# Two images' last layers side by side in a four-image, four-layer network kernel

## The chip, the cores and the metric

The kernel runs on one core of a Trainium2 chip. The measure is the device time of one execution in microseconds (us), here the median of three runs. The program takes all four images in one launch, in fp32.

The engines are named as in the profile: PE is TensorE's matrix products and PEld its loads of weights, DVE is VectorE, ACT is ScalarE, POOL is GpSimd, and SP is SyncE, which here mostly issues transfers. Each engine takes its own instructions strictly in the order in which the program lists them, and waits on semaphores for what other engines make.

## What is computed

An input of 4 x 32 x 32 x 384 goes through four residual layers, each of the form x + f(gn(x)), where gn is a group norm over 32 groups:

```python
# layer 0: deformable attention, 6 heads of 64, with a sampled position bias
offset = tanh(einsum('bhwc,ct->bhwt', gelu(ln(conv(q))), w_offp)) * [H/2, W/2]
xs = bilinear_sample(xg, offset + ref)
attn = softmax(q @ (xs @ w_k).T * scale + bilinear_sample(rpe, disp))
x = x + (attn @ (xs @ w_v)) @ w_out
# layer 1: attention, 12 heads of 32, weighted by similarity to group centres
sim = sigmoid(beta + alpha * l2norm(xg) @ l2norm(gc).T)
attn = softmax(q @ k.T * scale) * ((sim @ sim.T) * gamma + 1 - gamma)
x = x + (attn / (attn.sum(axis=2) + 1e-8) @ v) @ Wproj
# layer 2: box sums, 5 along W and 20 along the channels
s, d = box5(xn), box20(box5(xn * xn))
x = x + box20(s * s) / (d * norm)
# layer 3: 3 x 3 outlook attention
attn = softmax((xn @ Wa + ba).reshape(B, H, W, 9, 9))
x = x + fold3x3(attn @ patches3x3(xn @ Wv))
```

An image has 1024 tokens (N) of 384 channels (C), kept as three blocks (KC = 3) of 128 partitions by 1024. Images do not depend on each other.

## The kernel before

Two classes hold the work of an image. `Front` does layer 0; `Trunk` does layers 1, 2 and 3. A front leaves its result in a DRAM tensor `x1[b % 2]` (L489 and L495 store it), and a trunk loads it from there. Image 0's front runs by itself. From then on `Net.layer3` (L293) runs the trunk of image b with the front of image b + 1 woven in. Both are Python generators: each `yield` hands back a number of units for the work just issued, and the order of these yields is the order in which every engine gets its instructions. A trunk has 1109 units (`TRUNK_STEPS`): 15 for the norm, 158 for `inputs1`, 118 for each of six pairs, 18 for `out1`, 93 for `layer2`, 117 for `layer3`. A front has 714 (`FRONT_STEPS`). `done` counts the trunks in whole images and `ahead` the fronts; after each trunk step, front steps are issued until `ahead` is at least `done + LEAD`, with LEAD = 0.1. So the front of the next image is through when a trunk stands at 0.9 of its units, in its layer 2. After image 2's trunk there is no front left, and image 3's trunk runs alone.

The stages of a trunk, in order:

- `start` (L1285) loads `x1` into the buffer `whole` (three transfers on SP) and the matrix `gmat`, which sums over the groups, into a weight slot. For image b + 1 it is called in image b's `layer3`, at L2005, before the last products of that layer.
- `image` (L1292): the group norm, in place. Its statistics are on DVE (L328, L329), a product with `gmat` on PE (L362), a square root on ACT (L378) and the normalisation on DVE (L386).
- `layer1` (L1306): `inputs1` (L1319) makes queries, keys, values and group features (L407, L1356, L421), the first denominators and the similarities (L1572). Then six `pair`s (L1586) of heads follow: L1518 scores for the row sums, L1653 scores, L1661 exponentials on ACT, L1683 group weights, L1690 their product on DVE, L1625 the product with the values. A pair's result goes to the DRAM tensor `yd`; pair 5 reads the results of the earlier pairs back into `q4`, `k4` and `xg`, and its own result goes to `xg` by L1732 at its end.
- `layers23` (L1734) opens a pool for the remaining scopes. In it `out1` (L1742) loads x again, multiplies by `Wproj` (L1757) and adds (L1769). `layer2` (L1775) has the norm, box sums along W on DVE (L1792, L1811 to L1816), transposes into PSUM (L1799) and box sums over the channels as products with a band matrix (L1824); the quotient goes through ACT (L1839, L1840, L1849, L1850) and DVE (L1844 to L1867). `layer3` (L1872) has the norm, the 81 attention logits (L1889), their softmax (L1914, L1916), the values (L421), a product with `sel` (L1954), a passage through DRAM that turns the 3 x 3 attention into a band of tokens (`skew`, L1987, and `mt`, L1989), the band products (L2012) and the stores (L2021).

What the two streams share: the weight tiles of 128 x 3 x 384 come from one pool of three slots, in the order of the calls of `weights` (L253, on SP's queue); PSUM has two "big" buffers of 128 x 1024 and four "bank" buffers of 128 x 512. Box sums, transposes, scores and dense products take "big"; nearly all else takes "bank". Front tiles live on one side of SBUF and trunk tiles on the other. `whole` is a single buffer in the pool `keep`, used by each image in turn.

In the front, a half-head has eight steps of bias (L906, L907, L911, L912), score products (L918) with DVE additions (L921, L925), a row maximum, then L951, L952 and the products with the values (L953); a front has 12 half-heads. Its end is the division by the denominators, the output projection (the L407 products with `qpad` as left operand) and the stores to `x1`. It begins with norm, query, convolution, positions, gathers on POOL, and the key and value products (L407, L421).

Of the kernel before, what the change touches and what calls it, by code (L numbers as in the profile page):

```python
# [27 lines left out]
NB, HW, C = 4, 32, 384  # L28
N = HW * HW
KC = C // P  # L30
# [29 lines left out]


EARLY = (12, 0, 14, 8, 8)
TRUNK_STEPS, FRONT_STEPS, LEAD = 1109.0, (714.0, 714.0, 714.0), 0.1


def bc(ap, axis, n):
# [7 lines left out]
class Net:  # L74
# [217 lines left out]

    def layer3(self, b, out):  # L293

        for w in self.trunk.image(b, out):
            self.done += w / TRUNK_STEPS
            while self.ahead < self.done + LEAD:
                self.ahead += next(self.fronts, 1.0)
        assert self.ahead >= min(b + 1, NB - 1)


class Lane:
# [937 lines left out]
class Early(Front):  # L1240
# [14 lines left out]
    def begin(self, b):  # L1255
        nc = self.nc
        with self.scope("l0p"), self.tc.tile_pool(
            name=self.nm("l0w"), bufs=2, side=self.side
        ) as self.wts:
            self.qpad = self.wt([P, KC, PW, PW], "qpad")  # L1260
            nc.gpsimd.memset(self.qpad, 0.0)
            xh = yield from self.normed(b)
            for ko in range(KC):
                self.project(xh, ko, self.wq)
                yield
            self.taps[1] = self.conv_weights(1)
            oT = self.wt([P, KC, 2, N // 2], "a12", 2)
            for k in range(KC):
                yield from self.convolve(oT, k)
            nc.sync.dma_start(self.qp1, self.qpad.rearrange("p k y x -> p (k y x)"))  # L1270
            nc.sync.dma_start(self.of1, oT.rearrange("p k g n -> p (k g n)"))


class Trunk(Lane):
# [15 lines left out]
        self.begun = x, self.weights("gmat")  # L1290

    def image(self, b, out):  # L1292
        x, gmat = self.begun
        self.norm(x, x, None, gmat)
        self.xh = x
        yield 15
        with self.scope("l1y"):


            self.q4, self.k4 = self.wt([P, N], "q4"), self.wt([P, N], "k4")  # L1300
            self.xg = self.wt([P, N], "xg")
            yield from self.layer1(b)
            yield from self.layers23(b, out)


    def layer1(self, b):  # L1306
# [279 lines left out]
    def pair(self, p):  # L1586
# [5 lines left out]
        qa, ka = self.qks[p % 2]  # L1592
        sim = self.sim
        if p == 5:

            for k, t in enumerate((self.q4, self.k4, self.xg[0:64, :])):
                nc.sync.dma_start(t, self.yd[k * P : k * P + t.shape[0], :])
# [130 lines left out]
        y = self.wt([P, 512], "y")  # L1728
        nc.scalar.copy(y, av)
        out = self.yd[p * 64 : (p + 1) * 64, :] if p < 5 else self.xg[64:P, :]  # L1730
        for h in range(2):
            nc.sync.dma_start(out[:, h * 512 : (h + 1) * 512], y[64 * h : 64 * h + 64, :])  # L1732

    def layers23(self, b, out):  # L1734
        with self.scope("l23"):
            whole, self.x = self.whole()
            self.spare = whole[:, KC * N :].rearrange("p (y x) -> p y x", y=HW)
            yield from self.out1(b)
            yield from self.layer2()
            yield from self.layer3(b, out)  # L1740

    def out1(self, b):  # L1742
        nc, v = self.nc, self.nc.vector
        for k in range(KC):
            nc.scalar.dma_start(self.x[:, k, :], self.x1[b % 2][k * P : (k + 1) * P, :])
        w = self.weights("Wproj")
        y = (self.q4, self.k4, self.xg)
        self.mv = [self.moments() for _ in range(2)]

        ps = {}  # L1750

        def part(ko, ks):
            if ko not in ps:
                ps[ko] = self.big()
            for h in range(2):
                for ki in ks:
                    nc.tensor.matmul(  # L1757
                        ps[ko][:, h * 512 : (h + 1) * 512],
                        w[:, ki, ko * P : (ko + 1) * P],
                        y[ki][:, h * 512 : (h + 1) * 512],  # L1760
                        start=ki == 0,
                        stop=ki == KC - 1,
                    )

        part(0, (0, 1))
        part(1, (0, 1))
        for ko in range(KC):
            part(ko, (2,) if ko < 2 else (0, 1, 2))
            v.tensor_tensor(self.x[:, ko, :], ps[ko], self.x[:, ko, :], ALU.add)  # L1769
            self.stats(self.mv[0], self.x, ko)  # L1770
            yield 6
# [100 lines left out]
    def layer3(self, b, out):  # L1872
        nc, v = self.nc, self.nc.vector
        skew = self.skew[b % 2]
        with self.scope("l3"):
# [5 lines left out]
            w = self.weights("Wv")  # L1881
# [120 lines left out]
                    )  # L2002
                nc.scalar.copy(ys[:, i], pt[:, 0:C])
            yield 20
            if b + 1 < NB:  # L2005
                self.start(b + 1)
            for i in range(NJ):
                ps = self.bank()
# [10 lines left out]
                y = ys[:, i]  # L2019
# [87 lines left out]
```

## Time and profile before

| | |
|---|---|
| runs, median of 3 | 4391.65 us (4374.2 to 4397.6) |
| profiled execution | 4362.05 us |
| its span, first to last instruction | 4360.0 us |
| mean granted TensorE clock | 0.950 |
| transfers over the span | 391.18 MB, mean 90 GB/s |

The largest groups of instructions on the page, in the form "line, engine, operation, out <- in, shapes, count, then busy time and mean duration, then idle time of the engine just ahead of them with what ended it":

```profile
L1683 PE MATMUL bank<-whole,sg 128*128 128x512 f32 (+3 forms) x2304 | 850.1, 499 | 2.5 <-POOL sg L1636 1.0
...
L1690 DVE SCALAR_TENSOR_TENSOR e<-bank,gam,e 128x512 f32<-128x512 f32 x768 | 560.0, 747 | 304.5 <-PE bank L1683 188.0
...
L1653 PE MATMUL big<-qa,ka 64*128 64x512 f32 x1536 | 454.9, 672 | 85.6 <-ACT big L1528 82.4
...
L953 PE MATMUL bank<-lg,va 128*128 128x512 f32 x576 | 270.2, 611 | 12.8 <-ACT lg L952 12.8
...
L907 DVE SCALAR_TENSOR_TENSOR z<-win,bias_f,z 128x528 f32<-128x528 f32 x288 | 214.6, 762 | 20.6 <-ACT z L906 19.1
```

PE is the engine that is busiest. L1683 and L1653 belong to layer 1's pairs, L953 and L907 to layer 0's half-heads. Mean durations are times from start to end of one instruction; products overlap on PE, so that a group's busy time is less than its count times its mean.

### The profile page before, as it was taken

How to read it: one execution, taken by the hardware profiler on the slowest of the kernel's cores; microseconds unless marked ns; L12 is line 12 of the kernel's file. 1: busy time of each engine (PE TensorE's matmuls, PEld its weight loads, DVE VectorE, ACT ScalarE, POOL GpSimd, SP SyncE). 2: the span in 40 equal slices, each digit the busy share in tenths (PEclk: the TensorE clock that was granted, in tenths of full speed). 3: DMA queues.
4: the chain of work that ended last, by engine and by line, in shares of the span. 5: the costliest groups of instructions: out<-in, count | busy, mean ns of one | idle time of the engine just before them, and what ended most of it. 6: DMA issues, size and time to landing. Idle time of an engine off the chain costs nothing.

```text
span 4360.0 us, 45308 instructions
## 1 busy us (share of the span) xinstructions
PE 3915.6 (90%) x14832; PEld 1676.8 (38%) x14832; DVE 3107.4 (71%) x5902; ACT 2305.8 (53%) x3640; POOL 962.7 (22%) x979
## 2 busy tenths in 40 slices
PE   5888889998999898989899989899989989999998
PEld 3333433333334443433333444333333334344444
DVE  3599676878787547687878746678787874566654
ACT  3266445666674334576666433366675641566633
POOL 0655242112121105221212101431121301000000
PEclk8999989999999998999999999899999999999999
DMA  8744253123221255321222145432221214311111
GB/s 183 237 124 123 83 175 104 47 57 88 60 77 49 85 162 161 104 66 41 81 60 81 40 143 142 140 104 63 55 83 44 78 33 137 103 40 28 33 33 44
DMA packets 297461, 391.18 MB, mean 90 GB/s; under 512 B 168002, under 2 KB 229710, under 8 KB 296714
## 3 DMA queue, kind: packets, MB, share of 16 engines
q1 hardware_dynamic: 244826, 221.57, 18.1%
q0 software_dynamic: 39936, 145.53, 11.0%
q10 hardware_dynamic: 12464, 21.19, 1.5%
q8 instruction: 118, 1.93, 0.2%
q14 instruction: 117, 0.96, 0.1%
HBM read 300.15 MB, written 88.32 MB: 89 GB/s over the span
## 4 chain that ended last, share of the span: by engine, by line
PE 48%; DVE 26%; ACT 9%; issue 9%; DMA 4%; POOL 4%; SPq 0%; ACTq 0%; DVEq 0%; POOLq 0%
PE bank L1683 10%; PE big L1653 6%; PE big L407 5%; DVE nmax L1527 4%; DVE e L1690 3%; PE bank L953 3%; ACT big L1528 3%; PE bank L421 3%; PE big L1518 3%; POOL gat L769 2%; PE bank L1678 2%; PE bank L1625 2%; DVE z L1072 2%; DVE z L907 2%; PE big L656 2%
## 5 line engine op out<-in xcount | busy, mean ns | idle before, releaser
L1683 PE MATMUL bank<-whole,sg 128*128 128x512 f32 (+3 forms) x2304 | 850.1, 499 | 2.5 <-POOL sg L1636 1.0
L1690 DVE SCALAR_TENSOR_TENSOR e<-bank,gam,e 128x512 f32<-128x512 f32 x768 | 560.0, 747 | 304.5 <-PE bank L1683 188.0
L1528 ACT ACTIVATE big<-big,nmax 128x1024 f32<-128x1024 f32 x384 | 417.5, 1087 | 295.3 <-DVE nmax L1527 293.5
L1683 PEld LDWEIGHTS bank<-whole,sg 128*128 128x128 f32 x2304 | 399.4, 196 | 349.7 <-issue 273.5
L1653 PE MATMUL big<-qa,ka 64*128 64x512 f32 x1536 | 454.9, 672 | 85.6 <-ACT big L1528 82.4
L1527 DVE TENSOR_REDUCE nmax<-big 128x1 f32<-128x1024 f32 x384 | 452.3, 1217 | 61.4 <-PE big L1518 61.2
L1661 ACT ACTIVATE e<-big 128x1024 f32<-128x1024 f32 x384 | 381.8, 1020 | 175.4 <-PE big L1653 165.3
L894 POOL DMA_INDIRECT win<-strips,widx x288 | 312.8, 1086 | 702.7 <-DVE z L907 384.6
L1636 POOL TENSOR_SCALAR sg<-whole,gam 128x512 f32<-128x512 f32 x192 | 150.9, 786 | 1336.4 <-PE bank L1683 1058.3
L1518 PE MATMUL big<-k,q 32*128 32x512 f32 x1536 | 271.7, 657 | 41.7 <-ACT big L1528 31.3
L953 PE MATMUL bank<-lg,va 128*128 128x512 f32 x576 | 270.2, 611 | 12.8 <-ACT lg L952 12.8
L1653 PEld LDWEIGHTS big<-qa,ka 64*128 64x128 f32 x1536 | 147.2, 198 | 345.8 <-ACT big L1528 178.5
L769 POOL DMA_INDIRECT gat<-pairs,sidx x192 | 213.3, 1111 | 301.3 <-DVE ix_one L548 165.0
L912 DVE SCALAR_TENSOR_TENSOR lg<-z,bias_f,lg 128x512 f32<-128x512 f32 x288 | 216.6, 769 | 49.1 <-ACT lg L911 47.4
L906 ACT ACTIVATE z<-win,bias_f 128x528 f32<-128x528 f32 x288 | 205.4, 736 | 58.1 <-DVE lg L912 26.5
L951 DVE TENSOR_TENSOR lg<-lg,tb 128x512 f32<-128x512 f32 x288 | 182.0, 690 | 74.5 <-ACT tb L944 74.5
L907 DVE SCALAR_TENSOR_TENSOR z<-win,bias_f,z 128x528 f32<-128x528 f32 x288 | 214.6, 762 | 20.6 <-ACT z L906 19.1
L1625 PE MATMUL bank<-e,vs 128*32 128x512 f32 x1536 | 211.6, 619 | 15.9 <-DVE vs L1619 15.9
L1695 ACT COPY gn<-bank 128x128 f32<-128x128 f32 (+2 forms) x288 | 106.3, 370 | 208.5 <-DVE e L1690 207.6
L911 ACT ACTIVATE lg<-z,bias_f 128x512 f32<-128x512 f32 x288 | 199.9, 717 | 17.0 <-DVE z L907 13.8
L921 DVE TENSOR_TENSOR lg<-bank,lg 128x512 f32<-128x512 f32 x288 | 191.2, 682 | 11.7 <-PE bank L918 11.0
L918 PE MATMUL bank<-qs,kz 64*128 64x512 f32 x288 | 169.4, 672 | 12.4 <-DVE e L1690 9.0
(321 smaller groups left out, 6301.1 us busy)
## 6 DMA issues: line engine op xcount, KB each, us to landing
q<-qd SPq DMA_DIRECT2D x48, 256.0 KB
xg<-xgd SPq DMA_DIRECT2D x48, 256.0 KB
w<-in_gmat SPq DMA_DIRECT2D x16, 576.0 KB
pairs<-gat SPq DMA_DIRECT2D x48, 192.0 KB
w<-in_w_off SPq DMA_DIRECT2D x12, 576.0 KB
w<-in_Wqkv SPq DMA_DIRECT2D x12, 576.0 KB
a<-in_x SPq DMA_DIRECT2D x16, 384.0 KB
x<-a ACTq DMA_DIRECT2D x4, 1536.0 KB
```

What stands on the lines that cost most here:

```text
L769: pin(nc.gpsimd.indirect_dma_start(out=gat[:, g].rearrange("p l c -> p (l c)"), out_offset=None, in_=pairs[:, :], in_offset=bass.IndirectO ...
L894: nc.gpsimd.indirect_dma_start(out=win, out_offset=None, in_=self.strips[:, :], in_offset=bass.IndirectOffsetOnAxis(ap=self.widx[:, q, c : ...
L907: v.scalar_tensor_tensor(z, wv[:, 1 : HH + 1, 0 : HW + 1], sc(0, 1), z, ALU.mult, ALU.add)
L953: nc.tensor.matmul(po, self.values_of(h, j), lf, start=j == 0, stop=j == NJ - 1)
L1518: nc.tensor.matmul(ps[r][:, h * 512 : (h + 1) * 512], self.q4[rows, i * P : (i + 1) * P], self.k4[rows, 0:512], start=True, stop=True,)
L1527: v.tensor_reduce(nmax[:, r, i : i + 1], ps[r], AX.X, ALU.max, negate=True)
L1528: nc.scalar.activation(ps[r], ps[r], AF.Exp, bias=nmax[:, r, i : i + 1], accum_out=den[:, r, i : i + 1],)
L1625: nc.tensor.matmul(av[r0 : r0 + HD1, :], vs[:, r, :], es[h][:, r, :], start=j == 0, stop=j == NJ - 1,)
L1653: nc.tensor.matmul(ps[:, r, :], ka[rows, j * P : (j + 1) * P], qa[rows, cols], start=True, stop=True,)
L1661: nc.scalar.activation(e, ps, AF.Exp)
L1683: last = nc.tensor.matmul(ps[:, (mid - i0) * P :], sg[:, r, m, :], sim[:, h, r, m, (mid - i0) * P :], start=m == 0, stop=m == 1,)
L1690: v.scalar_tensor_tensor(e[:, r, :], ps, self.gam[:, 1:2], e[:, r, :], ALU.add, ALU.mult, accum_out=tot[:, r, h : h + 1],)
```

## The change

The diff, cut to its core:

```diff
@@ -60,7 +60,8 @@
 
 
 EARLY = (12, 0, 14, 8, 8)
-TRUNK_STEPS, FRONT_STEPS, LEAD = 1109.0, (714.0, 714.0, 714.0), 0.1
+TRUNK_STEPS, FRONT_STEPS, LEAD = 1109.0, (714.0, 714.0, 800.0), 0.1
+AHEAD = 20.0
 
 
 def bc(ap, axis, n):
@@ -292,11 +293,32 @@
 
     def layer3(self, b, out):
 
-        for w in self.trunk.image(b, out):
-            self.done += w / TRUNK_STEPS
-            while self.ahead < self.done + LEAD:
-                self.ahead += next(self.fronts, 1.0)
-        assert self.ahead >= min(b + 1, NB - 1)
+        if b + 1 < NB:
+            work = self.trunk.begin(b) if b + 2 == NB else self.trunk.image(b, out)
+            for w in work:
+                self.done += w / TRUNK_STEPS
+                while self.ahead < self.done + LEAD:
+                    self.ahead += next(self.fronts, 1.0)
+            assert self.ahead >= b + 1
+            if b + 2 == NB:
+                for _ in self.fronts:
+                    pass
+                self.first = self.trunk.end(b, out)
+            return
+
+
+        second = Trunk(self, "right")
+        with self.tc.tile_pool(name="keep2", bufs=1, side="right") as second.keep:
+            second.work = second.keep
+            second.start(b)
+            done = ahead = 0.0
+            for part in (second.begin(b), second.end(b, out)):
+                for w in part:
+                    done += w * 0.6 if second.late else 0.0
+                    while second.late and ahead < done + AHEAD:
+                        ahead += next(self.first, 1e9)
+            for _ in self.first:
+                pass
 
 
 class Lane:
@@ -1290,17 +1312,32 @@
         self.begun = x, self.weights("gmat")
 
     def image(self, b, out):
+        yield from self.begin(b)
+        yield from self.end(b, out)
+
+    def begin(self, b):
         x, gmat = self.begun
         self.norm(x, x, None, gmat)
         self.xh = x
+        self.late = False
         yield 15
+        self.scopes = ExitStack()
+        self.scopes.enter_context(self.scope("l23"))
+        self.mv = [self.moments() for _ in range(2)]
         with self.scope("l1y"):
 
 
             self.q4, self.k4 = self.wt([P, N], "q4"), self.wt([P, N], "k4")
             self.xg = self.wt([P, N], "xg")
             yield from self.layer1(b)
-            yield from self.layers23(b, out)
+            whole, self.x = self.whole()
+            self.spare = whole[:, KC * N :].rearrange("p (y x) -> p y x", y=HW)
+            yield from self.out1(b)
+
+    def end(self, b, out):
+        yield from self.layer2()
+        yield from self.layer3(b, out)
+        self.scopes.close()
 
 
     def layer1(self, b):
@@ -1592,6 +1629,8 @@
         qa, ka = self.qks[p % 2]
         sim = self.sim
         if p == 5:
+            self.late = True
+        if p == 5:
 
             for k, t in enumerate((self.q4, self.k4, self.xg[0:64, :])):
                 nc.sync.dma_start(t, self.yd[k * P : k * P + t.shape[0], :])
@@ -1731,21 +1770,12 @@
         for h in range(2):
             nc.sync.dma_start(out[:, h * 512 : (h + 1) * 512], y[64 * h : 64 * h + 64, :])
 
-    def layers23(self, b, out):
-        with self.scope("l23"):
-            whole, self.x = self.whole()
-            self.spare = whole[:, KC * N :].rearrange("p (y x) -> p y x", y=HW)
-            yield from self.out1(b)
-            yield from self.layer2()
-            yield from self.layer3(b, out)
-
     def out1(self, b):
         nc, v = self.nc, self.nc.vector
         for k in range(KC):
             nc.scalar.dma_start(self.x[:, k, :], self.x1[b % 2][k * P : (k + 1) * P, :])
         w = self.weights("Wproj")
         y = (self.q4, self.k4, self.xg)
-        self.mv = [self.moments() for _ in range(2)]
 
         ps = {}
 
@@ -2002,7 +2032,7 @@
                     )
                 nc.scalar.copy(ys[:, i], pt[:, 0:C])
             yield 20
-            if b + 1 < NB:
+            if b + 2 < NB:
                 self.start(b + 1)
             for i in range(NJ):
                 ps = self.bank()
```

What it does:

- The last front's units are divided by 800 instead of 714, so that `ahead` grows more slowly for each of its steps and more of them are issued per trunk step of image 2. What is left of the front when image 2's `begin` is done is issued there; by the count, nothing is.
- `image` is cut in two. `begin` has the norm, layer 1 and `out1`; `end` has `layer2` and `layer3`. The pool of `layers23` is opened at the start of `begin`, the two sets of moments are taken there, and the tiles `q4`, `k4` and `xg` are released after `out1`.
- Images 0 and 1 run as before. For image 2 only `begin` runs; its `end` is kept as a generator, `self.first`.
- Image 3 is run by a second `Trunk` whose tiles lie on the side that the last front has left, with a `whole` of its own in the pool `keep2`. Its `start`, norm, `inputs1` and pairs 0 to 4 run alone. At the head of pair 5 `late` becomes true. From then on each step of w units adds 0.6 w to `done`, and steps of image 2's `end` are issued until their units are at least `done + 20`. Image 2's 210 units are thus spread over image 3's pair 5, `out1`, `layer2` and `layer3`; whatever is left then is issued after it.
- `start(b + 1)` inside `layer3` is left for images 0 and 1 alone (`b + 2 < NB`), so image 3's loads are issued once, by the second trunk, right after image 2's `out1`.

No product, transfer or elementwise operation is added to or taken from the work of an image; the instructions are placed in another order, and in other buffers.

## The prediction

> **What bounds the kernel now.** I read the page's sums and slices first, then busy time by stretch around images 2 and 3, then TensorE's timeline in those stretches.
>
> ```profile
> PE 3915.6 (90%) x14832; PEld 1676.8 (38%) x14832; DVE 3107.4 (71%) x5902; ACT 2305.8 (53%) x3640; POOL 962.7 (22%) x979
> ...
> PE   5888889998999898989899989899989989999998
> ...
> PEclk8999989999999998999999999899999999999999
> ```
>
> PE is the bound: 3915.6 of 4360.0 us, nearly full in every slice. What PE does not use (444 us) lies at the start, between images and in the last slice. A change that only reorders work can win back such idle time and stretches at a lower clock, nothing else.
>
> ```profile
> core 0: us, PE busy (x) PEld busy (x) DVE busy (x) ACT busy (x) POOL busy (x), PEclk, DMA share, GB/s
> 2785.00:3503.00 718.00, 653.85 (x2576) 268.95 (x2573) 572.58 (x1131) 450.04 (x718) 155.14 (x155) 0.96 0.24 71
> 3503.00:3669.00 166.00, 146.84 (x432) 69.33 (x432) 97.87 (x157) 54.49 (x71) 13.44 (x9) 0.95 0.26 82
> 3669.00:3768.00 99.00, 94.66 (x289) 40.27 (x287) 47.69 (x78) 40.32 (x66) 8.20 (x15) 0.98 0.43 136
> 3768.00:4144.00 376.00, 371.20 (x1747) 155.91 (x1751) 245.43 (x557) 235.97 (x375) 27.69 (x40) 1.00 0.13 33
> 4144.00:4215.00 71.00, 71.00 (x344) 33.03 (x338) 35.69 (x108) 30.67 (x44) 5.56 (x8) 1.00 0.06 18
> 4215.00:4360.00 145.00, 114.48 (x342) 57.27 (x338) 67.97 (x105) 39.31 (x45) 11.36 (x7) 0.88 0.16 49
> 4229.90:4297.30 67.40, 47.54 (x106) 21.31 (x106) 45.62 (x57) 28.04 (x26) 9.08 (x4) 0.86 0.06 18
> 4297.30:4360.00 62.70, 52.08 (x198) 29.59 (x198) 17.18 (x40) 10.69 (x18) 1.82 (x2) 0.88 0.25 76
> ```
>
> The rows are: image 2's six pairs with front 3 beside them; image 2's out1, layer 2 and layer 3 with the rest of front 3; image 3's norm and inputs1; its pairs 0 to 4; its pair 5; its out1, layers 2 and 3 together; its layer 2 alone; its layer 3 alone. Image 3's pairs fill PE (371.20 of 376, all 71 of 71). The last 145 us do not: 30.5 us idle, and the rest at 0.88, which costs 114.48 x 0.12 = 13.7 us more. So 44 us could be won there at most. The stretch 3503 to 3669 has 19 us idle and 7 by the clock.
>
> ```profile
> start us, us, engine line op out<-in xcount [idle before <-releaser]
> 3501.74 1.07 PE L1625 MATMUL bank<-e,vs 128*32 128x512 f32 x8 [0.32 <-DVE vs L1619]
> ...
> 3607.49 5.33 PE L407 MATMUL big<-qpad,w 128*128 128x512 f32 x12
> ...
> 3669.24 1.62 PE L362 MATMUL bank<-gn_mv,w 128*128 128x2 f32 x14
> 3672.99 17.39 PE L407 MATMUL big<-whole,w 128*128 128x512 f32 x36 [2.12 <-DVE whole L386]
> ...
> 3768.05 2.19 PE L1653 MATMUL big<-qa,ka 64*128 64x512 f32 x8 [0.26 <-issue]
> ...
> 4214.01 1.07 PE L1625 MATMUL bank<-e,vs 128*32 128x512 f32 x8
> ...
> 4228.84 1.02 PE L1757 MATMUL big<-xg,w 128*128 128x512 f32 x2
> 4233.19 2.74 PE L362 MATMUL bank<-gn_mv,w 128*128 128x2 f32 x14 [3.33 <-DVE gn_mv L358]
> 4242.11 3.75 PE L1799 MATMUL big<-t,ident 128*128 128x512 f32 x4 [6.19 <-ACT sq L1789]
> ```
>
> These are the joints: image 2's pairs end at 3502.8, front 3 ends at 3612.8, image 3's norm starts at 3669.2, its pair 0 at 3768.05, its last pair ends at 4215.1, out1 at 4229.9; the span ends at 4360.
>
> **The change as a sum.** I cut the new span at those joints: 3502.8 + F + S + 447.0 (image 3's pairs, 3768.05 to 4215.1, which the change leaves alone up to pair 5) + 144.9 (4215.1 to 4360) + E. F is what front 3's remainder costs when it moves into image 2's pairs; S is the way from the end of image 2's pairs to image 3's pair 0, now 265.3 us; E is what image 2's layers 2 and 3 add to image 3's pair 5 and tail.
>
> F. With 800 units, front 3 is through at 714/800 - 0.1 = 0.7925 of image 2's 1109 units, unit 879, inside pair 5. By counts after 3503, the remainder is 32 of 192 L953 products (15.60 us), 16 of 192 L918 (5.87), 36 L407 of the output projection (17.75) and about 3.4 of small products: 42.6 us of PE. About 10.5 of 12 half-heads ran inside the pairs, so 1.5 move. Lower bound: PE's own time for 1.5 half-heads (60.80 us busy in L918 over the 11 and 75.29 in L953 over the 10 that ran in the pairs: 5.5 + 7.5 = 13.0 each) and the projection: 1.5 x 13.0 + 17 = 36. Upper: what a half-head costs among pairs as they run: the pairs take 718 beside it and 447.0 alone, less 30 us for front 3's two value and key products, over 10.5: 23.0 us each; 1.5 x 23.0 + 17.75 = 52. Those two products now also stand ahead of pair 0, beside the gathers of 2700 to 2785, where the clock is 0.83: 30 x (1/0.83 - 1/0.96) = 5 more, 57. I take 45, near the plain PE sum, because DVE is idle 145 of the 718 us and PE 64.
>
> S. What is left in it is out1 (4215.1 to 4229.8: 14.7), the norm's small product (1.6), 2.1 of wait as before, and 3672.99 to 3768.05 (95.1): 114. On SP, image 3's first two x loads go early, the third is queued behind L1732's stores of pair 5's y; it is due before the end of out1 and three statistics (1.3 us each) follow it. The weight gmat is there already. Bounds 110 and 125 (the third load and the norm's chain of 3.3 + 6 us bare); I take 116. So the joint shrinks by 265.3 - 45 - 116 = 104 us, out of which E is paid.
>
> E. The work moved is one image's layers 2 and 3: alone they take 4229.9 to about 4357, 127 us, with 47.54 us of PE at clock 0.86 (41 at full clock) in layer 2 and 52.08 at 0.88 (46) in layer 3. Layer 2 goes beside pair 5. Its 45.62 us of DVE and 28.04 of ACT have room there (35.69 and 30.67 of 71 are taken). Its 41 us of PE have none, and extend the pair one for one. I add 9 us there: the norm's chain (6.19 and 3.33 us of PE idle above) and box sums that share the two "big" PSUM buffers with the pair's score products. Layer 3's 46 us stand beside image 3's out1, layer 2 and layer 3, where 44 us can be won at most; since layer 3 itself waits much (10.6 of its 62.7 us are idle), I take 18 won: 28. E = 41 + 9 + 28 = 78. Bounds: 43 (87 less all 44) and 127 (nothing hidden). At the lower clock of the last row the removed idle time would itself raise the load, which is why I stay off the lower end.
>
> Other edits. layer3 no longer loads image 3's x and gmat (L2005): three transfers and one, hidden in either place. gmat for image 3's layer 3 takes the weight slot of layer 2's band, so it loads only after the last box sum and, on SP, behind image 2's skew and mt transfers. In the trace, gmat took 6.28 us to land and the chain before its use is 5.6 us; if the cover is gone, it costs 0 to 8 us, and the L362 product, the L386 normalisation and all of image 3's layer 3 are late behind it. I take 0 here, since image 2's layer 3 has products to give PE meanwhile. A second set of buffers costs no time.
>
> Table loads on ACT. In layer 2 the row is:
>
> ```profile
> 4236.58 1.28 ACT L378 ACT_TABLE_LOAD   x1 [20.86 <-DVE gn_rstd L375]
> 4237.88 0.30 ACT L378 ACTIVATE gn_rstd<-gn_rstd,eps 128x3 f32<-128x3 f32 x1
> ```
>
> Eight such loads now fall among pair 5's exponentials: 8 x 1.28 = 10.3 us of ACT, and with 30.67 + 28.04 us of work in a stretch of some 120 us it is covered, so I add nothing. The Trainium skill, "ScalarE: Activation LUTs", section "What ACT_TABLE_LOAD costs", gives 2.66 us for a switch, of which 1.38 is a drain after the load, and its section on table sets advises against alternating; here the activation starts 0.02 us after the load ends, and no drain shows. By the page the loads would take 21 us, and an estimate from it that put the extra 11 on the path would make E 89.
>
> Sum: 3502.8 + 45 + 116 + 447.0 + 144.9 + 78 = 4333.7, 26 us under 4360.0. The profiled execution took 4362.05, 2.05 more than its span, and the median of the runs is 4391.65, 1.0068 times that: (4333.7 + 2.05) x 1.0068 = 4365.
>
> **The rivals.** A, the forecast: E between about 60 and 100: 4345 to 4388.
> B, no change: the front's remainder was hidden beside layers 2 and 3 and is not hidden among the pairs (F = 57), and S is 125 since out1 alone covers the norm: 4354.7, or 4386. For it: DVE with 80% and PE with 91% in image 2's pairs. Against: 19 us of PE idle beside layers 2 and 3.
> C, slower: the two images' streams serialise. Engines take their queues in order, and a box sum that waits for ACT or DVE holds pair 5's next product on PE. Price: E = 127 + 8 with the late gmat = 135: 4390.7, or 4423. It decides from E = 126 (0.5% slower); equal times are at E = 104. For it: layer 2's chain leaves PE idle 6.19, 3.33 and 5.60 us at a time even when alone. Against: beside front 3, PE was busy 146.84 of 166 us.
> D, better: E = 52, F = 36, S = 113: 4295.7, or 4327. For it: the idle time of the tail and the low clock are there to be filled; against: the box sums' and the softmax's chains stay in their order.
> That the change does not do what it says I exclude: in the order of instructions on PE the front's last products stand among image 2's pair 5, image 2's layer 2 among image 3's pair 5, and its layer 3 among image 3's out1 to layer 3.
>
> **How the numbers follow.** A change of 0.5%, 22 us, is what can be told from none. Chances: A 0.44 (of which 0.34 faster, 0.10 within), B 0.18, C 0.22, D 0.16. Faster 0.34 + 0.16 = 0.50; within 0.18 + 0.10 = 0.28; slower 0.22. The range runs from D's end to C's price, 4318 to 4424; the forecast's own is 4345 to 4388.
>
> **What would show it.** Right: the L407 products with qpad before the last L1625 of image 2; 111 to 120 us from there to image 3's first L1653; about 121 us for image 3's pair 5 in place of 71; about 173 from its end to the span's end with the clock over 0.95. Wrong: image 2's pairs longer by over 57; idle PE in pair 5 before L1799 or L1824 over 15 us; a tail over 200; the L362 of image 3's layer 3 waiting for gmat.

## The result and the profile after

The changed kernel takes 4406.47 us (median of 19 runs, 4397.46 to 4424.3) against 4392.76 us for the kernel before (19 runs beside it): a ratio of 1.0039, 95% interval 1.0029 to 1.005. It is slower by 0.4%, where 0.6% faster was forecast.

First the page of the changed kernel: busy time of the engines, then PE and its clock in 40 slices.

```profile
PE 3932.0 (89%) x14832; PEld 1682.2 (38%) x14832; DVE 3105.0 (70%) x5902; ACT 2303.5 (52%) x3638; POOL 963.9 (22%) x979
...
PE   5888888988999898989899989788888999999998
...
PEclk8899989999999998999999999899998999999999
```

PE has the same 14832 products and is busy 16.4 us longer than in the profile of before. By itself that says little: two executions of one and the same kernel (e5 and e5b below) differ by 10.8 us in it. Slices 26 to 31 (2753 to 3414 us: image 2's pairs and the end of the way to them) now all have a digit below 9, where before only 26 and 30 had one.

The profiled execution took 4407.51, its span is 4405.3. The profile of before was a lucky one (4362.05, under all 19 runs): up to about 2540 us both kernels issue the same PE instructions, and the changed one is already 19 us late at 2465 us. So I profiled the kernel before once more (e0, span 4386.2) and count from the end of image 1's pairs in each kernel. The next two blocks give busy time by stretch, first for e0, then for the changed kernel: image 2's norm and inputs1; its pairs; from there to image 3's pair 0; the rest (for the changed kernel split into pairs 0 to 4, pair 5, tail).

```profile
2674.90:2811.50 136.60, 119.88 (x402) 51.11 (x400) 99.16 (x177) 56.11 (x94) 62.05 (x63) 0.89 0.49 149
2811.50:3529.60 718.10, 648.72 (x2577) 269.79 (x2576) 574.30 (x1131) 451.82 (x719) 153.22 (x154) 0.97 0.25 71
3529.60:3793.90 264.30, 241.30 (x724) 109.85 (x720) 145.45 (x235) 95.26 (x137) 21.73 (x24) 0.97 0.31 102
3793.90:4386.20 592.30, 555.77 (x2425) 245.60 (x2425) 348.93 (x770) 305.72 (x462) 44.41 (x55) 0.97 0.13 35
```

```profile
2679.70:2858.00 178.30, 146.41 (x423) 66.10 (x419) 110.72 (x194) 56.65 (x98) 62.76 (x63) 0.88 0.45 140
2858.00:3607.70 749.70, 676.98 (x2582) 276.19 (x2582) 590.84 (x1158) 464.66 (x740) 151.81 (x150) 0.95 0.22 65
3607.70:3733.20 125.50, 111.33 (x319) 47.46 (x320) 58.28 (x101) 42.11 (x68) 8.44 (x17) 0.95 0.43 138
3733.20:4109.00 375.80, 371.28 (x1747) 155.89 (x1751) 246.02 (x558) 236.00 (x375) 27.93 (x40) 1.00 0.13 33
4109.00:4230.60 121.60, 116.21 (x451) 51.28 (x443) 74.55 (x159) 59.58 (x70) 19.03 (x13) 1.00 0.06 20
4230.60:4405.30 174.70, 153.02 (x540) 79.35 (x536) 82.30 (x145) 48.24 (x62) 11.38 (x7) 0.95 0.24 75
```

The columns are length, PE, PEld, DVE, ACT and POOL busy (with counts), PE's clock, DMA share and GB/s. The joint between the images shrank by 139 us (149 were planned), and image 3's pair 5 and tail pay 80 for it. But image 2's norm and inputs1 take 42 us longer and its pairs 32. PE's idle time in the last stretch hardly fell: 36.5 us of 592.3 before, 31.6 of 672.1 after.

The joints of the changed kernel on PE's timeline:

```profile
3597.69 5.33 PE L429 MATMUL big<-qpad,w 128*128 128x512 f32 x12
...
3606.64 1.06 PE L1664 MATMUL bank<-e,vs 128*32 128x512 f32 x8
...
3620.47 5.98 PE L1787 MATMUL big<-xg,w 128*128 128x512 f32 x8 [7.43 <-DMA xg<-y]
...
3637.54 17.98 PE L429 MATMUL big<-whole,w 128*128 128x512 f32 x36 [4.48 <-issue]
...
4324.92 3.12 PE L384 MATMUL bank<-gn_mv,w 128*128 128x2 f32 x14 [7.85 <-DMA w<-in_gmat]
```

The front's last products now stand ahead of the last pair's (so the change does what it says), out1 waits 7.43 us for pair 5's own result, and image 3's layer 3 waits 7.85 us for its gmat. Before, out1 had no such wait, and the product with gmat waited 5.78 us (e0), for the statistics and not for the matrix.

### The profile page after: what moved, and what is told of

It is laid out like the page before. It is cut to its first block, busy times and chain, and to the rows that moved or that the text cites. A ratio compares the mean times of both kernels' runs of the same rounds, so it can differ in the third digit from the quotient of the medians.

```text
span 4405.3 us, 45238 instructions
## 1 busy us (share of the span) xinstructions
PE 3932.0 (89%) x14832; PEld 1682.2 (38%) x14832; DVE 3105.0 (70%) x5902; ACT 2303.5 (52%) x3638; POOL 963.9 (22%) x979
## 5 line engine op out<-in xcount | busy, mean ns | idle before, releaser
L1555 PE MATMUL big<-k,q 32*128 32x512 f32 x1536 | 282.2, 661 | 51.8 <-ACT big L1565 20.5
```

Source lines behind the costliest of these rows:

```text
L1555: nc.tensor.matmul(ps[r][:, h * 512 : (h + 1) * 512], self.q4[rows, i * P : (i + 1) * P], self.k4[rows, 0:512], start=True, stop=True,)
```

## The experiments

All lengths are from the profiles, in us. "To pair 0" is from the end of image 1's pairs to image 2's pair 0; "joint" from the end of image 2's pairs to image 3's pair 0; "rest" from there to the end of the span. Ratios are to before in the same series (medians of before in the four series: 4392, 4371, 4405 and 4387, so that only ratios compare).

| kernel | to pair 0 | pairs of image 2 | joint | rest | ratio (95%) |
|---|---|---|---|---|---|
| before, again (e0) | 346.7 | 718.1 | 264.3 | 592.3 | 0.9985 (0.9962 to 1.0008) |
| changed | 395.5 | 749.6 | 125.5 | 672.1 | 1.0039 (1.0029 to 1.0050) |
| e1 paced | 356.1 | 778.9 | 122.3 | 675.3 | 0.9980 (0.9961 to 0.9999) |
| e2 800 alone | 398.5 | 750.8 | 241.6 | 594.3 | 1.0116 (1.0078 to 1.0155) |
| e3 held back, 714 | 346.4 | 716.4 | 190.0 | 672.8 | 1.0002 (0.9985 to 1.0019) |
| e4 even | 384.8 | 727.3 | 123.9 | 672.2 | 1.0057 (1.0041 to 1.0073) |
| e5 = e1 + gmat | 344.7 | 778.8 | 125.2 | 668.2 | 0.9964 (0.9948 to 0.9980) |
| e6 = e1 + y on POOL | 344.2 | 777.6 | 124.8 | 672.7 | 0.9981 (0.9969 to 0.9994) |
| e8 = e1, not woven | 341.1 | 774.6 | 124.1 | 714.6 | 1.0062 (1.0042 to 1.0082) |
| e9 layer 3 alone | 355.8 | 732.2 | 217.0 | 633.0 | 1.0007 (0.9992 to 1.0021) |
| e10 = e9, slower | 352.2 | 728.3 | 218.1 | 633.8 | 1.0010 (0.9994 to 1.0025) |
| e11 = e5, earlier end | 346.3 | 778.7 | 114.6 | 668.4 | 0.9975 (0.9958 to 0.9993) |
| e5 again (e5b) | 346.8 | 780.0 | 123.9 | 668.1 | 0.9981 (0.9965 to 0.9998) |

### e0: the kernel before, once more

> The kernel before, profiled once more. The profile of before (4362.05 us) lies near the lower end of its runs (4374 to 4399), that of the changed kernel (4407) at its median. Up to 2540 us both kernels issue the same instructions, and yet the changed one is 16 us later at 520 us and 19 us later at 2465 us. If that is a matter of the execution, the stretch 104 to 520 us of this profile may fall anywhere between the two; if it comes from the change (other addresses of buffers), it is within 3 us of the first profile's 416 us.

Its span is 4386.2, 26 us over the first profile's, and image 1's pairs end at 2464.9, against 2443.2 there and 2462.6 in the changed kernel. The stretch named in the expectation took 416.0 us in the first profile, 428.0 in e0 (105.8 to 533.8 us) and 432.9 in the changed kernel. So the 19 us are a matter of the execution, and e0 is the profile to compare with.

### e1: the front denser only from pair 0 on

```diff
-            self.fronts = (
-                w / FRONT_STEPS[i - 1] for i in range(1, NB) for w in self.front.layer0(i)
-            )
+            def fronts():
+                for i in range(1, NB):
+                    seen = 0
+                    for w in self.front.layer0(i):
+                        yield w / (834.0 if i == NB - 1 and seen >= 183 else 714.0)
+                        seen += w
+            self.fronts = fronts()
```

> The change, but front 3 keeps the pace 714 until pair 0 of image 2 (183 units) and goes at 834 from there, so that it ends in the same place. In the changed kernel the way from image 2's norm to its pair 0 took 45 us longer than before and its pairs 31 us longer, 86 in all with the 9 ahead of the norm. Theory P (place): what was pushed ahead of pair 0, the gathers above all, leaves PE waiting; then pair 0 starts where it did before, the pairs take 45 to 53 us longer, and the time is 25 to 40 us under the changed kernel's, about 4370, 0.5% faster than before. Rival D (density): a denser front costs over 23 us a half-head among the pairs wherever it stands; then the pairs take 75 us or more longer and the time is within 12 us of the changed kernel's.

Measured: 4386.15 us, 20 under the changed kernel's 4406.47. Both theories hold a part. The way to pair 0 is back to 356 (341 to 347 in e5, e6, e8, e11 and e5b, which have the same order up to there), so some 40 to 54 us of it were a matter of place. But the pairs take 60.8 longer, neither 45 to 53 nor 75. Here is where those go, PE's groups in image 2's pairs, for e0 and then for the changed kernel and e1:

```profile
L1683 PE MATMUL bank<-whole,sg 128*128 128x512 f32 (+3 forms) x576 | 213.3, 500 | 0.5
L1653 PE MATMUL big<-qa,ka 64*128 64x512 f32 x384 | 115.1, 670 | 28.7 <-ACT big L1528 27.9 <-ACT e L1661 0.8
...
L1625 PE MATMUL bank<-e,vs 128*32 128x512 f32 x384 | 53.2, 618 | 5.6 <-DVE vs L1619 5.6
...
L1518 PE MATMUL big<-k,q 32*128 32x512 f32 x320 | 51.9, 642 | 3.1 <-ACT e L1661 2.5 <-issue 0.6
```

```profile
L1722 PE MATMUL bank<-whole,sg 128*128 128x512 f32 (+3 forms) x576 | 217.4, 507 | 6.4 <-DVE lg L943 3.9 <-ACT gn L1734 1.5 <-DVE e L1729 0.6
L1692 PE MATMUL big<-qa,ka 64*128 64x512 f32 x384 | 124.9, 689 | 32.5 <-ACT big L1565 29.6 <-issue 2.6 <-DVE res L516 0.3
...
L1555 PE MATMUL big<-k,q 32*128 32x512 f32 x320 | 57.7, 639 | 6.1 <-ACT e L1700 5.4 <-ACT big L1565 0.6
...
L1664 PE MATMUL bank<-e,vs 128*32 128x512 f32 x384 | 55.0, 621 | 0.3 <-DVE vs L1658 0.3
```

```profile
L1726 PE MATMUL bank<-whole,sg 128*128 128x512 f32 (+3 forms) x576 | 213.0, 500 | 5.8 <-DVE lg L947 2.9 <-ACT gn L1738 2.0 <-DVE e L1733 0.5
L1696 PE MATMUL big<-qa,ka 64*128 64x512 f32 x384 | 120.8, 681 | 25.0 <-ACT big L1569 24.7 <-DVE res L520 0.3
...
L1668 PE MATMUL bank<-e,vs 128*32 128x512 f32 x384 | 58.0, 611 | 3.5 <-DVE vs L1662 3.5
L1559 PE MATMUL big<-k,q 32*128 32x512 f32 x320 | 57.0, 640 | 4.5 <-ACT big L1569 2.2 <-ACT e L1704 1.9 <-issue 0.2
```

These rows are not added up: a group's busy time counts the time in which at least one of its products runs, so products that overlap with another group's are counted in both. For the 1664 products of these four groups the sums are 433.5 us in e0, 455.0 in the changed kernel and 448.8 in e1, while the mean durations hardly differ between e0 and e1 (500 and 500, 670 and 681, 618 and 611, 642 and 640 ns). What has no such overlap is PE's busy time over the whole stretch, here for e1's pairs and for those of e11, a later version with nearly the same work in them:

```profile
2813.00:3591.80 778.80, 702.36 (x2674) 289.67 (x2674) 602.23 (x1176) 467.12 (x744) 153.97 (x154) 0.96 0.24 69
2795.00:3573.70 778.70, 694.58 (x2671) 290.92 (x2670) 607.22 (x1185) 466.20 (x744) 168.40 (x166) 0.97 0.26 73
```

Against e0's 648.72 us busy, e1 adds 53.6: the 42.6 of the products that moved in, and 11 more. Its idle time adds 7 (76.4 against 69.4). In the changed kernel the pairs add 11 us of products (those moved in, less those that now stand ahead of pair 0), 17 more of busy time and 3 of idle. PE's mean clock is 0.97 in e0, 0.95 in the changed kernel and 0.96 in e1; on some 700 us a hundredth is worth 7 us (an estimate), so the clock may account for most of the 17 in the changed kernel. It does not make the pairs of e1's order long: e11 has e0's clock, 0.97, and its pairs are as long as e1's, with less busy and more idle time. So the remainder costs some 60 us among the pairs, of which 42.6 are its own products; no run separates the rest further.

### e2: 800 units alone

```diff
-TRUNK_STEPS, FRONT_STEPS, LEAD = 1109.0, (714.0, 714.0, 714.0), 0.1
+TRUNK_STEPS, FRONT_STEPS, LEAD = 1109.0, (714.0, 714.0, 800.0), 0.1
```

> The kernel before with the last front's 800 units alone; image 2's layers 2 and 3 are not held back. If the cost lies in the front's pace and not in the held-back layers, image 2's pairs end 85 us later (less what differs between executions) as in the changed kernel, out1, layers 2 and 3 run bare in some 142 us instead of 166, and the time is about 4450, 60 us over before (1.014). If the pace costs only the 45 us of the prediction, it is about 4413 (1.005).

Measured: 4445.56, as the first theory says. Up to the end of image 2's pairs it is the changed kernel (1149 us against 1145, e0 1065), with nothing held back. And the joint tells what the front's remainder had cost in its old place: 264.3 - 241.6 = 23 us, beside layers 2 and 3.

### e3: held back, with the front at 714

```diff
-TRUNK_STEPS, FRONT_STEPS, LEAD = 1109.0, (714.0, 714.0, 800.0), 0.1
+TRUNK_STEPS, FRONT_STEPS, LEAD = 1109.0, (714.0, 714.0, 714.0), 0.1
...
-            assert self.ahead >= b + 1
```

> The change with the last front's units left at 714: its remainder runs bare after image 2's out1, ahead of image 3. Image 2's pairs then end where they did before. If a bare remainder costs its PE time and its division chain, 45 to 60 us, and image 3's start 125 us plus some 10 for its loads that now wait for the front, the way from the end of the pairs to image 3's pair 0 is 180 to 195 us, against 86 + 125 = 211 in the changed kernel counted from the same point: 16 to 30 us faster than the changed kernel, about equal to before. If the remainder bare costs over 86 us (row maximum, exponentials and division one after the other with nothing beside), it is slower than the changed kernel.

The joint is 190.0, 64.5 over the changed kernel's, so the remainder costs 65 bare, with what image 3's start then waits for it. That is less than the 80 it costs at 800, and the kernel is 12 us faster than the changed one, a little less than expected, and equal to before.

### e4: an even pace for all three fronts

```diff
-TRUNK_STEPS, FRONT_STEPS, LEAD = 1109.0, (714.0, 714.0, 800.0), 0.1
+TRUNK_STEPS, FRONT_STEPS, LEAD = 1109.0, (740.5, 740.5, 740.5), 0.1
```

> The change, but with all three fronts at 740.5 units (3 x 714 / 740.5 = 2.8925) in place of 714, 714 and 800: the last front ends at the same point of image 2, and each trunk takes a third of the extra front work. Seen so far: e0 (before) has image 2's pairs 1065 us after image 1's end, the changed kernel 1145, the paced one (e1) 1135, for 42.6 us of PE work moved. If the waste (27 to 38 us) grows with the density of the front among the pairs, an even pace loses little of it, some 10 us, and the time is 4365 to 4375, under e1's 4386 and before's 4392. If the waste is a fixed price of any shift, the time is within 8 us of e1's.

Both expectations fail: 1.0057, no better than the changed kernel and slower than e1. Image 2's pairs now cost only 9 us more than e0's, but image 1's pairs already end 41 to 50 us later than in e5, e6 and e8 of the same series (2485.6 against 2435.9 to 2444.6), and image 2's norm to its pair 0 takes 178.7 us as in the changed kernel. An even pace starts fronts 2 and 3 earlier against their trunks, and so front 3's gathers and first products again fall ahead of pair 0. The place of the front's stages against the trunk's counts, not only how dense they are.

### e5: a gmat of image 3's own

```diff
+            second.gm = second.keep.tile([P, KC, C], F32, tag="gm", name="gm")
...
-        self.begun = x, self.weights("gmat")
+        if self.gm is not None:
+            src = self.a["gmat"].rearrange("(k p) d -> p k d", p=P)
+            self.nc.sync.dma_start(self.gm, src)
+        self.begun = x, self.gm or self.weights("gmat")
...
-            self.norm(self.x, xh, self.mv[1])
+            self.norm(self.x, xh, self.mv[1], self.gm)
```

> e1 (the change with the paced front) with a buffer of its own for image 3's gmat, loaded once ahead of image 3's norm. In the changed kernel image 3's layer 3 waited 7.85 us for this matrix, whose load stands behind image 2's skew and mt transfers on SP and needs the band's slot. If that wait is what it looks like, the span from image 3's pair 0 to the end falls from 675 to 667 or 670 us and the time to about 4380. If the statistics chain behind it ends as late, nothing changes (within 2 us in that span).

The rest falls to 668.2, from 675.3 in e1 and 672.7 in e6, whose last stretch has the same work: 4.5 to 7 us, about what was expected. The row of the product that waited, in e5:

```profile
4271.15 3.15 PE L389 MATMUL bank<-gn_mv,gm 128*128 128x2 f32 x14 [2.74 <-DVE gn_mv L385]
```

Behind the wait for the matrix stood the statistics of image 3, 2.74 us later than PE's last product.

### e6: the last y on POOL's queue

```diff
+        eng = nc.gpsimd if p == 5 and self.b == NB - 2 else nc.sync
         for h in range(2):
-            nc.sync.dma_start(out[:, h * 512 : (h + 1) * 512], y[64 * h : 64 * h + 64, :])
+            eng.dma_start(out[:, h * 512 : (h + 1) * 512], y[64 * h : 64 * h + 64, :])
```

> e1 with image 2's last y (two transfers of 128 KB) on POOL's queue in place of SP's. In the changed kernel they took 12 us to land, behind image 3's x loads, Wg and out1's x, and out1 waited 7.43 us for them. If they wait in SP's queue of transfers, they land in some 3 us on another queue, and the stretch from the end of image 2's pairs to image 3's pair 0 falls from 122 to 115 or 117 us. If it is the 16 DMA engines that are full, they land no sooner, and the stretch stays within 2 us.

The joint did not fall (124.8 against 122.3 in e1), as the second theory says, yet the run does not prove it. POOL's timeline in e6:

```profile
3565.11 0.94 POOL L1511 MEMSET qa<- 32x1024 f32 x1 [39.45 <-DMA x<-res]
3566.00 0.94 POOL L1512 MEMSET ka<- 32x1024 f32 x1
3566.89 1.15 POOL L1776 DMA_DIRECT2D xg<-y  x2
```

The transfers were held on POOL behind two memsets of image 3 and left at 3566.9; PE had them at 3571.6, 4.7 us after, against 12.1 us from issue to use in the changed kernel. They were faster on the way and as late at the end (out1 waited 6.55 us). The Trainium skill, "DMA: Bandwidth & Descriptors", section "Issuing engines are not separate DMA queues", says that another issuing engine saves only issue time; this run cannot decide it, since the transfers also left later, when part of the loads was through. The changed kernel's own trace is nearer to an answer. Here is the busy share of its 16 DMA engines from 3600 to 3625 us, a digit for each 0.625 us:

```profile
DMA  0000007887754799999999999999883110000000
```

They were 90% or more busy from 3608.8 to 3617.5 us, that is for 8.7 of the 12.1 us from y's issue at 3608.4 to its use. So for that time the engines were full; whether the order in SP's queue cost anything besides is not shown.

### e8: layers 2 and 3 not woven in

```diff
-                    while second.late and ahead < done + AHEAD:
-                        ahead += next(self.first, 1e9)
+                    pass
```

> e1 with image 2's layers 2 and 3 not woven in at all: they run after image 3's. This prices the side-by-side run by itself: from image 3's pair 0 to the end it took 592 us in before and 675 in e1 (E = 83). The prediction's upper bound for E was 127, the time of both layers alone. If weaving them in is what hides them, E is 120 to 130 and the time some 4430. If the layers overlap in any order that is allowed, since image 2's do not depend on image 3's, E is under 100.

The rest is 714.6, E = 122 against 80: the first theory. The weaving itself wins 42 us.

### e9 and e10: only layer 3 held back

```diff
-TRUNK_STEPS, FRONT_STEPS, LEAD = 1109.0, (714.0, 714.0, 800.0), 0.1
+TRUNK_STEPS, FRONT_STEPS, LEAD = 1109.0, (714.0, 714.0, 718.0), 0.1
...
+            if b + 2 == NB:
+                work = (w for part in (self.trunk.begin(b), self.trunk.layer2()) for w in part)
...
-                    done += w * 0.6 if second.late else 0.0
+                    done += w * 0.4 if second.late else 0.0
```

(e10: 0.3 and AHEAD = 0.0; both with e5's gmat.)

> Only image 2's layer 3 is held back: its layer 2 stays beside front 3's remainder (718 units, so that the front ends with layer 2), where the remainder cost 24 us in before (166 us for the stretch, 142 for out1, layers 2 and 3 alone), against 60 to 85 us among the pairs and 65 bare. Layer 3 goes beside image 3's pair 5, out1, layers 2 and 3 (0.4 w, AHEAD 20), and image 3 has its own gmat as in e5. If it is the place of the front's remainder that undid the change, image 2's pairs end where before's do, image 3's pair 0 starts 40 to 50 us earlier than in before, pair 0 to the end takes 592 + 25 to 35, and the time is 15 to 25 us under before (0.9945). If image 3's norm waits for the front and its loads bare, pair 0 is only some 25 us earlier and the time is that of before.

> e9 with layer 3 of image 2 at 0.3 w and AHEAD 0: less of it beside pair 5, which PE fills, more of it beside image 3's layers 2 and 3, which leave PE idle. If idle time of the tail can be had at all, it is 5 to 10 us faster than e9; if the chains of the two images then end one after the other, it is up to 10 us slower.

Both are equal to before. The joint is 217, a gain of 47, but layer 3 beside image 3 costs 41 (rest 633.0), more than the 25 to 35 expected, and image 2's pairs ran 10 to 14 us longer than e0's. In e9 image 3's norm product waits 13.1 us with PE empty, for the statistics of x, which the front has only just stored. A slower weave changes nothing (633.8), so at these two paces the pace in the tail is not what holds it. The 47 us of the joint nearly fit the expectation, but since pair 0 came only 24 us earlier from image 1's end (1305 against 1329), the second theory describes the outcome.

### e11: the front ends before pair 5 does

```diff
-                        yield w / (834.0 if i == NB - 1 and seen >= 183 else 714.0)
+                        yield w / (909.0 if i == NB - 1 and seen >= 183 else 714.0)
```

> e5 (paced front, image 3's own gmat) with front 3 at 909 in place of 834 units from image 2's pair 0, so that it ends some 60 units earlier in the middle of pair 5. Image 3's x and the next weights are then loaded under pair 5 and no longer together with image 2's last y. If the 6 to 7 us that out1 waits for that y, and part of the 4.5 us ahead of image 3's first products, are this collision of transfers, the way from the end of image 2's pairs to image 3's pair 0 falls from 125 to 112 to 117 us; the pairs hold the same work and should cost no more than 3 us extra: 6 to 10 us faster than e5. If the denser front costs more among the pairs (theory D), the gain is eaten there.

> e5 once more beside e11 on the same chip: 0.996 of before as it was, with 125 us from the end of image 2's pairs to image 3's pair 0 and 668 us from there to the end.

The joint falls to 114.6, the pairs stay (778.7 against 780.0), and e11 ends 10.8 us earlier than e5b from image 1's pairs. SP's queue in the changed kernel shows what is avoided:

```profile
3603.05 0.32 SPq L1311 DMA_DIRECT2D whole<-x  x1
...
3604.80 0.39 SPq L1311 DMA_DIRECT2D whole<-x  x1
3605.23 0.58 SPq L258 DMA_DIRECT2D w<-in_Wg  x1
3608.38 1.14 SPq L1771 DMA_DIRECT2D xg<-y  x2
3613.72 0.33 SPq L1311 DMA_DIRECT2D whole<-x  x1
```

The front's end releases image 3's loads 5 us ahead of y, and y lands when they are through. In e11 the x loads go out under pair 5, and the first wait left in the joint is 3.19 us for the norm:

```profile
3593.26 17.39 PE L434 MATMUL big<-whole,w 128*128 128x512 f32 x36 [3.19 <-DVE whole L413]
```

The medians say it less clearly: 4380.83 against 4384.08 of e5b, with ratios whose intervals overlap. e5 (0.9964 and 0.9981) and e11 (0.9975) are versions faster than both kernels, by 0.2 to 0.4% against before.

## Why the prediction was wrong

Its sum was F + S + E, with S and the rest of the span cut at the same joints. Measured against e0:

| term | forecast | bounds | measured |
|---|---|---|---|
| F, front 3's remainder moved into image 2's norm to pairs | 45 | 36 to 57 | 80.4 (1145.1 - 1064.7) |
| S, joint | 116 | 110 to 125 | 125.5 |
| E, layers 2 and 3 beside image 3 | 78 | 43 to 127 | 79.8 (672.1 - 592.3) |

**F is the step that failed:** "I take 45, near the plain PE sum, because DVE is idle 145 of the 718 us and PE 64." It is 35 of the 47 us by which the three terms miss. I took PE's and DVE's idle time in the pairs as room for more front. It was not room: from the end of image 1's pairs to the end of image 2's PE is busy 958.3 us in e0 and 1019.2 in the changed kernel, and idle 106.4 and 125.9. The 80.4 are thus the 42.6 us of moved products in full, 18 us of further busy time and 20 us of further idle time, and for the last two the forecast's 45 left 2. The row I had, 23 us for each half-head among pairs, was the nearer one and gives 52 for F; e1, whose pairs keep what they had and take the remainder, pays 61 there (56 to 62 in e5, e6, e8, e11 and e5b). Why PE's busy time grows by more than the products that came in is only in part known: at the changed kernel's clock of 0.95 against 0.97 in the pairs the estimate above gives 14 us, but e11's pairs are 61 longer than e0's at e0's clock of 0.97. What makes up the rest stays open.

The rest is place: "30 x (1/0.83 - 1/0.96) = 5 more" for the products now ahead of pair 0. The stretch there grew by 42: its PE time by 26.5 (31.5 of those products came in, and 72 products of the front's convolution, 8.0 us in e0, moved ahead of image 2's norm, where the stretch grew by 7) and its idle time by 15. The waits of PE from norm to pair 0 show why, e0 first:

```profile
PE big L1518 <- ACT big L1528: 10.9, 3, 9.9
PE bank L1396 <- ACT sq L1394: 2.0, 1, 2.0
```

```profile
PE big L1555 <- issue: 7.8, 3, 5.4
PE bank L819 <- DVE xn L807: 6.9, 2, 6.2
PE big L1555 <- ACT big L1565: 6.5, 3, 4.5
PE bank L819 <- DVE sq L1481: 4.2, 1, 4.2
```

L819 turns the gathered samples. With more of the front ahead of pair 0, PE reaches these transposes before the samples are there and, in order, holds the trunk behind them: 11.0 us of waits that e0 does not have. In all, idle time went from 17 to 32 us.

**S** missed by 9.5. I named the third x load behind y as the danger; it was y itself that came late, while the loads for image 3 that the front's end had released, together with out1's own, filled the DMA engines. Had I asked what the earlier end of the front would trigger, the new collision was there to be seen; e11 shows it by taking it away.

**E** was right, as a sum and in its parts: pair 5 about 121 (121.6), tail about 173 (174.7). Layer 2's PE work does extend a full pair: pair 5 grew by 50.6 us, and PE's busy time in it by 45. The two layers run bare cost 122 (e8). The gmat wait was taken as 0 of 0 to 8; it was 7.85 us, of which 4.5 to 7 could be won. "I take 0 here, since image 2's layer 3 has products to give PE meanwhile" went wrong by the order and not by a lack of products:

```profile
4316.52 0.55 PE L2030 MATMUL big<-ident,whole 128*128 128x128 f32 x3 [1.69 <-DVE xp L1896]
4324.92 3.12 PE L384 MATMUL bank<-gn_mv,w 128*128 128x2 f32 x14 [7.85 <-DMA w<-in_gmat]
```

At 4317 us image 2's layer 3 still had 24 of its 48 value products and all 44 of its band products to come. They stood behind the waiting product in PE's order, since the norm issues all its steps without a `yield` at which the weave could put others in between.

**The rivals.** In mechanism B came nearest: the remainder is not hidden among the pairs, and S is 125. Its F of 57 was too low, and so its time, 4386, by 20 us. C's time, 4423, is 17 us over the measured one, but by another way: a serial tail, which did not happen. (The recorded range begins at 4318; D's sum gives 4327, and nothing here rests on the difference.) What no case asked is what the remainder cost in its old place, 23 us (e2): there it and layers 2 and 3 covered each other, and parting them won 139 us of joint. The change pays 80 and 80 for it.

**The table loads** on ACT needed no term: eight of them, of 1.28 us each, stand in pair 5's stretch, as forecast, and it came out at the forecast length without one.

## What to carry to other kernels

When a change takes work from beside other work, price what stays behind without its cover and what arrives at the new place by the measured marginal cost of the same work there, not by the busiest engine's own time; idle per cents of a mixed stretch need not be free room. When two streams are woven by a counter, their phase matters as well as their density: pace each stage against the stage it is to lie beside. And where one stream ends earlier, look at what its end releases: the loads it sets free compete with the transfer that the other stream is waiting for.

## What the runs showed of the hardware

PE's granted clock differed by stretch: 1.00 in image 3's pairs alone, 0.97, 0.95 and 0.96 in image 2's pairs with the front in e0, the changed kernel and e1, 0.88 to 0.89 on the way to image 2's pair 0. The page "TensorE: Matmul & The Clock Gate" of the Trainium skill, section "HAM oscillation — how this bites in real kernels", gives the rule that PE should not idle over some 3.4 us; image 3's pairs 0 to 4, whose longest wait is 0.5 us in the changed kernel, show 1.00 here, and the stretch ahead of image 2's pair 0, with waits of up to 6.2 us there and 9.9 us in e0, 0.88 and 0.89. In image 2's pairs PE has one wait over 3.4 us in e0, three in e11 and four in the changed kernel, at clocks of 0.97, 0.97 and 0.95: that fits the rule in its direction, but does not give the size, and what lowers the clock there stays open.

Executions differ as well. The first front took 416.0 and 428.0 us in two executions of the kernel before (104.6 to 520.6 us and 105.8 to 533.8), and the median of before differed by 34 us between series, more than the effect of the change. That is why only ratios within a series, and lengths from one joint to the next, are compared here.
